# Graph attention on one core: adjacency factors as maxima on VectorE, a bias of 2 in GpSimd's exponentials, and opening zeros in one bf16 pass

## The chip, the cores and the metric

The kernel runs on one core of a Trainium2 chip. The core has engines that work side by side, each through its own queue in order: TensorE (PE in the profile, PEld for its weight loads), VectorE (DVE), ScalarE (ACT), GpSimd (POOL) and SyncE (SP), which here issues nearly all DMAs. Times are device microseconds of one execution; lower is better. A table row "L1272" is line 1272 of the kernel.

## The reference

x is 3327 x 128, adj is a 3327 x 3327 matrix of zeros and ones with ones on its diagonal. Two layers follow each other, each with a residual and a normalisation:

```python
# layer 0: one-head attention with leaky-relu scores, masked by adj
H = X @ W.T + b
e = leaky_relu(A * (H @ a_s) + A * (H @ a_r).T, 0.2)
x = layernorm(x + softmax(where(A > 0, e, NEG), axis=1) @ H)

# layer 1: heads and channels trade places, adj is added twice
q = (x @ Wq.T).reshape(d, n, h)          # d = 128, n = 3327, h = 8
# k and v likewise
a = einsum('dnh,dmh->dnm', q, k) * d ** -0.5 + adj + adj
out = einsum('dnm,dmh->dnh', softmax(a, axis=2), v).reshape(n, h * d) @ Wo.T
x = layernorm(x + out)
```

Layer 1 is nearly all the work: 128 score matrices of 3327 x 3327, an exponential for each of their elements, and a product with 8 value columns. With q scaled by half, the exponent is 2 * (s + adj), where s is the score of the kernel's matmul. So exp(2s + 2 adj) can be had in two ways: add adj to s and take the exponential with a scale of 2; or take exp(2s) and multiply it by a factor that is 1 where adj is 0 and e^2 where adj is 1.

## The kernel before, in words

The function `special` is what runs on these inputs; `general` is a way out for inputs that fail a test of ranges, and is not entered.

**Layer 1's loop.** The 128 matrices are handled in 32 groups of four (HG). The queries are cut into six blocks of 512 and a last one of 256 (`exact`). A pass over one block for one group of four is an entry of `sequence`; two groups share the short last block, side by side in one 512-wide tile ("shared block", `both` in the code, two entries in `s.v4`). So 16 pairs of groups x 13 entries give 208 entries, numbered u.

**One entry.** The keys are cut into 26 tiles of 128 or 127. A tile for four matrices is two "chunks" of 128 x 1024: scores of two matrices each, made by `pair_scores` (called from the loop, recorded under line 155) into a PSUM tile `scb`. Each chunk goes one of two ways:

- POOL's way (`at_ is None`): ScalarE takes exp(2s) from PSUM into SBUF (L1272), and GpSimd multiplies it by the factor (L1273). Its score tile comes from a pool of one buffer.
- DVE's way: VectorE adds adj to the scores (L1275), and ScalarE takes the exponential of both chunks of a tile at once, one round later, in place (`exp_late`, L1059).

Then `products` multiplies the four exponentials with the value columns and accumulates over the 26 tiles in the PSUM tile `av` (L1015), with a lag of five tiles. `av` has one buffer; VectorE copies it out at the end of the entry (L1025) and SP stores it.

**Rounds, stretches and the written order.** The order of all instructions is written out by hand (`manual_schedule`): nothing is moved by a planner afterwards. An entry has 26 rounds, each with two chunks. The rounds fall into "stretches" of three (`plans`, `laid`): a stretch has three tiles, two chunks of one of them go POOL's way, the other four DVE's way. In a stretch ScalarE therefore has two exponentials of 1024 elements and two of 2048. The first stretch of every second entry and the last of every entry are shorter.

**The adjacency tiles.** `want_adj(n)` loads what stretch n needs into a tile `at` with three planes (five buffers, issued three stretches ahead on SP's queue): plane 0 is for POOL's factor, the others are for DVE's additions. The first time that a pair of block and key tile is met (`made_by`), plane 0 holds raw adj, and `make_factor`, called at the end of the stretch before (L1283), turns it in place into 1 or e^2 = adj * (e^2 - 1) + 1 (L840). Whether GpSimd or VectorE does it depends on the stretch's number m in its entry; VectorE's form goes over the row in a strided order of two runs of 256. The result is stored to DRAM (`ftd`, L841, issued through `issue` a few rounds later on SP), and later entries load it from there (L807). There are 7 blocks x 9 = 63 such factors, all made in the first seven entries.

**Opening a shared block's sums.** In a shared block the four matrices of both groups lie side by side in `av`, and each matmul writes one half. `start=True` cannot be given by the halves here, so `products` first issues four matmuls over all 512 columns with a zero weight tile `nought` and the first tile of exponentials as the moving side (L1012), one per band of 32 output rows; all others then accumulate.

**Beside the loop.** Layer 0 for the later row tiles, the projections, the final products and normalisations are put between the rounds as small side jobs by `work` and `work_tensor` (matmuls recorded under L246, VectorE's L337, L419, L425 and others, GpSimd's L319 and L328). The prologue does layer 0 for the first rows; its ScalarE instructions L909, L931, L934 and L937 have a bias that is read per partition, and L941 a scale that is read per partition. ScalarE's L421 there has constants alone.

The constants `nought`, `ones` and the like are made in the pool `keep` before anything else (L195 to L198).

Of the kernel before, what the change touches and what calls it, by code (L numbers as in the profile page):

```python
# [8 lines left out]
F32 = mybir.dt.float32  # L9
F32R = mybir.dt.float32r  # L10
BF16 = mybir.dt.bfloat16
I32 = mybir.dt.int32
AF = mybir.ActivationFunctionType
ALU = mybir.AluOpType
# [3 lines left out]
P = 128  # L18
# [9 lines left out]
E2 = 7.38905609893065  # L28
# [19 lines left out]
def kernel(  # L48
# [27 lines left out]
    nc = tc.nc  # L76
# [24 lines left out]
    W = 512  # L101
# [51 lines left out]
    def special():  # L153
# [9 lines left out]
        with ExitStack() as sx, tc.manual_schedule(engines=ALL):  # L163
            keep = sx.enter_context(tc.tile_pool(name="sx_keep", bufs=1))
# [27 lines left out]
            nc.vector.memset(one_row, 1.0)  # L192
            nrm = keep.tile([1, 4], F32, name="nrm")

            nought = keep.tile([P, 32], F32, name="nought")  # L195
            nc.vector.memset(nought, 0.0)
            ones = keep.tile([P, 1], F32, name="ones")
            nc.vector.memset(ones, 1.0)  # L198

# [60 lines left out]
            def issue(f):  # L260
                pend.append([ISSUE, f])

            def tick(all_=False):
                for p in pend:
                    p[0] -= 1
                while pend and (all_ or pend[0][0] <= 0):
                    pend.pop(0)[1]()
# [561 lines left out]
            def make_factor(n):  # L829
                if n < len(stretches):  # L830
                    u, m = stretches[n]
                    b = sequence[u][1]
                    times, _ = plans[u % 2][m]
                    if times is None or made_by[b, times] != n:
                        return
                    w = exact[b][2]
                    f = adjs[n][:, 0, :w]
                    engine = nc.vector if m % 2 else nc.gpsimd
                    by = f if engine is nc.gpsimd else f.rearrange("p (b a) -> p a b", a=2)
                    engine.tensor_scalar(by, by, E2 - 1.0, 1.0, op0=ALU.mult, op1=ALU.add)  # L840
                    issue(lambda: nc.sync.dma_start(ftd[b][times // 3][:, :w], f))  # L841


# [2 lines left out]
            with ExitStack() as st:  # L846
# [7 lines left out]
                bias = pro.tile([P, 3], F32, name="bias")  # L854
# [36 lines left out]
                def mm():  # L891
                    return pps.tile([P, 512], F32, tag="mm", name="mm")

                b = mm()
                nc.tensor.transpose(b[:, :D], w0[:, :D], ident)
                nc.vector.tensor_copy(w0t, b[:, :D])
                b = mm()
# [6 lines left out]
                b = mm()  # L904
                nc.tensor.transpose(b[:, :P], first["x"], ident)
                nc.vector.tensor_copy(x0T, b[:, :P])
                b = mm()
# [97 lines left out]
            def products(s, i):  # L1005
                if s.left == NT:
                    s.av = pv.tile([P, W], F32, name="av")
                r, e, w = kr[i], s.e.pop(i), s.w
                s.left -= 1
                if s.left == NT - 1 and len(s.v4) > 1:  # L1010
                    for j in range(HG):
                        nc.tensor.matmul(s.av[32 * j : 32 * j + 32, :], nought[:r], e[:r, j, :], start=True, stop=False)  # L1012
                for j in range(HG):
                    for k, v4 in enumerate(s.v4):
                        nc.tensor.matmul(  # L1015
                            s.av[32 * j : 32 * j + 32, k * w : k * w + w],
                            v4[:r, j, i * H1 : i * H1 + 32],
                            e[:r, j, k * w : k * w + w],
                            start=(s.left == NT - 1 and len(s.v4) == 1),
                            stop=(s.left == 0 and k + 1 == len(s.v4)),  # L1020
                        )
                if s.left == 0:
                    o4 = op_.tile([P, W], F32, name="o4")
                    n0, c0, _ = exact[s.b]
                    nc.vector.tensor_copy(o4, s.av)  # L1025
                    for k, g in enumerate(s.gs):
                        for j in range(HG):
                            d = g * HG + j
                            issue(
                                lambda engine=nc.sync, j=j, d=d, at=k * w: engine.dma_start(  # L1030
                                    oT[:, d * N + n0 + c0 : d * N + n0 + w], o4[32 * j : 32 * j + H1, at + c0 : at + w]
                                )
                            )
# [183 lines left out]
            for u, (gs, b) in enumerate(sequence):  # L1217
                if len(gs) == 1:
                    groups = {g: x for g, x in groups.items() if g >= gs[0]}
                s = Block()  # L1220
                s.gs, s.b, s.q4, s.left, s.e, added = gs, b, queries[0], NT, {}, {}
                s.k4, s.v4 = [groups[g][0] for g in gs], [groups[g][1] for g in gs]
                w = s.w = exact[b][2]
                odd, both = u % 2, len(gs) == 2
                rounds, order, starts = plan_of[odd]
                for n, rnd in enumerate(rounds):
                    now = u * NR + n
                    if n in starts:
                        m = number[u, starts[n]]
                        if m:  # L1230
                            want_adj(m + AHEAD)
                        a = adjs[m]
                    tick()
                    for f in soon.pop(now, []):
                        f()
                    if opening < NG:
                        at = begins[opening] - OPEN[opening]
                        if now == at:
                            finish_to(("rows", reads[opening]), None)
                            tick(True)  # L1240
                            groups[opening] = open_group(opening)
                        if now >= at:
                            parts = groups[opening][2]
                            for k, f in enumerate(parts):
                                if now == at + OPEN[opening] * k // len(parts):
                                    f()
                        if now == begins[opening] - 1:
                            opening += 1
                    if u + 1 < len(sequence):
                        if n == NR // 2:  # L1250
                            queries = open_queries(u + 1)
                        if NR // 2 <= n < NR // 2 + HG:
                            queries[1](n - NR // 2)
                    sc = {}
                    for i, h, z in reversed(rnd) if n == 1 and not odd else rnd:
                        sc[i, h] = (pe if z is None else pd).tile([P, 2, 512], F32, name="scb")
                        for k, k4 in enumerate(s.k4):
                            c = slice(k * w, k * w + w)
                            for t in range(2):
                                pair_scores(sc[i, h][: kr[i], t, c], k4, s.q4[:, c], i, kr[i], 2 * h + t, w)  # L1260
                    work_tensor(now, n, odd, both)
                    for i, _, _ in reversed(rnd):
                        if i not in s.e:
                            s.e[i] = sp.tile([P, HG, W], F32, name="e4")
                    for i, h, at_ in rnd:
                        r, z = kr[i], sc[i, h]
                        eh, z = s.e[i][:r, 2 * h : 2 * h + 2, :], z[:r]
                        if both:
                            eh, z = (x.rearrange("p t (k w) -> p (t k) w", w=w) for x in (eh, z))
                        ah = a[:r, at_ or 0, :w].unsqueeze(1).to_broadcast([r, W // w * 2, w])  # L1270
                        if at_ is None:
                            nc.scalar.activation(eh, z, AF.Exp, scale=2.0)  # L1272
                            nc.gpsimd.tensor_tensor(eh, eh, ah, op=ALU.mult)  # L1273
                        else:
                            nc.vector.tensor_tensor(eh, z, ah, op=ALU.add)  # L1275
                            added.setdefault(i, []).append(h)
                    exp_late(now)
                    for i in [i for i, hs in added.items() if len(hs) == 2 or odd and i == NT - 2]:
                        hs = added.pop(i)
                        late.append((now + 1, s, i, 2 * min(hs), 2 * max(hs) + 2))  # L1280
                    if n + 1 in starts or n + 1 == NR:
                        del adjs[m]
                        make_factor(m + 1)  # L1283
                    waiting.append((s, order[n]))
                    multiply(n, odd)
                    work(now, n, odd, both)
# [386 lines left out]
```

## Time and profile before

| | us |
|---|---|
| median of 3 runs | 9910.65 (9908.4 to 9919.17) |
| the profiled execution's own time | 9913.75 |
| its span | 9911.7 |
| ScalarE busy | 9826.0 (99%) |
| TensorE busy | 9247.0 (93%) |
| VectorE busy | 9144.8 (92%) |
| GpSimd busy | 9121.1 (92%) |
| POOL's way, exponential L1272: 3640, mean of one | 1.219 |
| DVE's way, exponential L1059: 3640, mean of one | 2.088 |
| POOL's product L1273: 3640, mean of one | 2.399 |
| DVE's addition L1275: 7176, mean of one | 1.219 |

A line of the groups reads: line, engine, operation, output tile <- input tiles, their shapes, count | busy time in us, mean of one in ns | idle time of the engine just before them, and what ended most of it. A line of the list in order of time reads: start and duration in us, engine, line, operation, tiles and shapes, count, and in brackets the idle time before it and its releaser; neighbours of one kind are merged. A line of the waits reads: who waited <- for whom: us in total, times, longest. Instructions of one engine can overlap in the records: the next one starts before the one in front has left the engine's pipe. Then the durations add up to more than the time, and the step from start to start is what an instruction costs the engine.

### The profile page before, as it was taken

The page shows a single profiled execution, that of the slowest core. Times are in us where ns is not written, and L with a number is a line of the kernel's source. Part 1 is how long each engine was busy: PE and PEld are TensorE (multiplying, and loading weights), DVE is VectorE, ACT ScalarE, POOL GpSimd, SP SyncE. Part 2 cuts the span into 40 slices and gives each one's busy share as a digit, 9 for nine tenths or more (in the row PEclk, how much of TensorE's full clock was granted, in tenths as well). Part 3 has the DMA queues.
Part 4 walks back from the last instruction along what each step waited for, and adds up shares of the span by engine and source line. Part 5 has one row for each costly group of instructions (what it writes and reads, how often), then busy time and mean ns, then how long its engine had stood idle before and what let it go on. Part 6 is the DMA issues. An engine that isn't in the chain of part 4 may idle for free.

```text
span 9911.7 us, 205795 instructions
## 1 busy us (share of the span) xinstructions
PE 9247.0 (93%) x79785; PEld 2990.5 (30%) x79785; DVE 9144.8 (92%) x9996; ACT 9826.0 (99%) x7349; POOL 9121.1 (92%) x4643
## 2 busy tenths in 40 slices
PE   8999999999999999999999999999999999999998
PEld 3323323233232332323223232232322323223232
DVE  8999999999989999999999999999999999998988
ACT  8999999999999999999999999999999999999999
POOL 7999998999889999989998998989998999998888
PEclk9999999999999999999999999999999999999999
DMA  7665555655656556555565655556555565555554
GB/s 215 189 185 171 171 179 163 186 158 171 184 154 180 171 162 186 169 167 173 160 184 166 182 172 168 166 166 183 168 172 174 156 181 171 175 172 156 168 152 135
DMA packets 1344016, 1699.58 MB, mean 171 GB/s; under 512 B 347980, under 2 KB 641782, under 8 KB 1339060
## 3 DMA queue, kind: packets, MB, share of 16 engines
q1 hardware_dynamic: 1341726, 1685.40, 56.7%
q8 instruction: 628, 10.29, 0.4%
q14 instruction: 360, 2.95, 0.1%
q10 hardware_dynamic: 1302, 0.95, 0.0%
HBM read 1581.93 MB, written 103.93 MB: 170 GB/s over the span
## 4 chain that ended last, share of the span: by engine, by line
ACT 51%; PE 20%; issue 11%; POOL 7%; DVE 4%; DMA 1%; SPq 0%; POOLq 0%; DVEq 0%; ACTq 0%
ACT e L1059 36%; ACT e L1272 15%; PE av L1015 9%; PE scb L155 9%; POOL e L1273 7%; DVE e L1275 3%; PE bank L246 2%; DVE o L1025 1%; DMA at<-in_adjT_dram 0%; POOL w L319 0%; POOL w L328 0%; DMA k4b<-kT 0%; SPq L781 0%; PE av L1012 0%; DVE dump L337 0%
## 5 line engine op out<-in xcount | busy, mean ns | idle before, releaser
L1273 POOL TENSOR_TENSOR e<-e,at 128x1024 f32<-128x1024 f32 x3640 | 8678.3, 2399 | 728.5 <-ACT e L1272 685.6
L1275 DVE TENSOR_TENSOR e<-scb,at 128x1024 f32<-128x1024 f32 (+1 forms) x7176 | 8442.1, 1219 | 699.3 <-PE scb L155 542.9
L1059 ACT ACTIVATE e<-e 128x2048 f32<-128x2048 f32 (+2 forms) x3640 | 7599.5, 2088 | 15.3 <-DVE e L1275 14.5
L1015 PE MATMUL av<-e,v4b 128*32 128x512 f32 (+2 forms) x46592 | 5737.0, 572 | 44.1 <-DVE o L1025 25.6
L1272 ACT ACTIVATE e<-scb 128x1024 f32<-128x1024 f32 x3640 | 4435.9, 1219 | 25.3 <-PE scb L155 23.6
L155 PE MATMUL scb<-q4b,k4b 32*128 32x512 f32 (+2 forms) x23296 | 3667.8, 476 | 599.3 <-ACT e L1272 505.9
L155 PEld LDWEIGHTS scb<-q4b,k4b 32*128 32x128 f32 (+1 forms) x23296 | 1657.2, 189 | 5388.0 <-ACT e L1272 3382.1
L1015 PEld LDWEIGHTS av<-e,v4b 128*32 128x32 f32 (+1 forms) x46592 | 1100.9, 108 | 1185.2 <-issue 888.3
L246 PE MATMUL bank<-hsb,w 128*32 128x129 f32 (+1 forms) x5200 | 277.9, 286 | 0.0
L319 POOL TENSOR_SCALAR w<-trow,er 128x129 f32<-128x129 f32 x650 | 234.6, 386 | 23.6 <-DMA trow<-td 22.8
L337 DVE TENSOR_SCALAR_CACHE_REDUCE dump<-a 128x384 bf16<-128x384 f32 (+2 forms) x468 | 247.4, 529 | 0.6
L328 POOL TENSOR_TENSOR w<-w,a 128x384 f32<-128x384 f32 (+3 forms) x225 | 211.1, 938 | 6.1 <-DVE e L1275 6.1
L246 PEld LDWEIGHTS bank<-hsb,w 128*32 128x32 f32 (+1 forms) x5200 | 102.3, 108 | 157.7 <-issue 157.7
L1025 DVE COPY o<-av 128x512 f32<-128x512 f32 x208 | 141.8, 682 | 4.6 <-PE av L1015 4.6
L419 DVE TENSOR_SCALAR hi<-bank 128x256 fp32r<-128x256 f32 (+1 forms) x200 | 83.4, 417 | 10.7 <-DMA kT<-hi 8.6
L246 PE MATMUL bank<-wo,ot 128*32 128x128 f32 x1600 | 85.2, 285 | 0.0
L425 DVE SCALAR_TENSOR_TENSOR lo<-bank,hi 128x256 fp32r<-128x256 f32 (+1 forms) x200 | 83.1, 416 | 0.0
L246 PE MATMUL bank<-wq,x1T 128*32 128x256 f32 x800 | 64.7, 395 | 0.0
L246 PE MATMUL bank<-wk,x1T 128*32 128x256 f32 x800 | 64.3, 393 | 0.0
L246 PE MATMUL bank<-wv,x1T 128*32 128x256 f32 x800 | 63.9, 391 | 0.0
L523 PE MATMUL bank<-ident,o 128*128 128x128 f32 x225 | 52.0, 303 | 0.0
L246 PEld LDWEIGHTS bank<-wo,ot 128*32 128x32 f32 x1600 | 31.5, 108 | 48.5 <-issue 48.5
(140 smaller groups left out, 678.5 us busy)
## 6 DMA issues: line engine op xcount, KB each, us to landing
at<-in_adjT_dram SPq DMA_DIRECT2D x1536, 512.0 KB
at<-ftd SPq DMA_DIRECT2D x1674, 256.0 KB
at<-in_adjT_dram SPq DMA_DIRECT2D x278, 256.0 KB
k4b<-kT SPq DMA_DIRECT2D x124, 415.9 KB
q4b<-qT SPq DMA_DIRECT2D x1532, 32.0 KB
at<-in_adjT_dram SPq DMA_DIRECT2D x192, 224.0 KB
a<-in_adjT_dram SPq DMA_DIRECT2D x50, 504.0 KB
at<-ftd SPq DMA_DIRECT2D x135, 128.0 KB
```

Source lines behind the costliest of these rows:

```text
L155: nc.tensor.matmul(dst, k4[32 * j : 32 * j + H4, first_key(i) : first_key(i) + 2 * r - 1 : 2], q4[32 * j : 32 * j + H4, :nb], start=True, ...
L246: nc.tensor.matmul(dst[c0:c1], w[:, c0:c1], mov, **kw)
L319: nc.gpsimd.tensor_scalar(w, s["t"][:, :, :T3], -LOWEST, e, op0=ALU.min, op1=ALU.max)
L328: nc.gpsimd.tensor_tensor(w, w, s["a"][n][:, c0 - i0 : c1 - i0, :r], op=ALU.mult)
L337: nc.vector.tensor_scalar(z, a, float(k), None, op0=ALU.is_equal, op1=ALU.add, accum_out=even[:, t, at : at + 1])
L419: nc.vector.tensor_scalar(s["hi"][:r], s["b"][:r, :QW], scale, None, op0=ALU.mult)
L1015: nc.tensor.matmul(s.av[32 * j : 32 * j + 32, k * w : k * w + w], v4[:r, j, i * H1 : i * H1 + 32], e[:r, j, k * w : k * w + w], start=(s.l ...
L1025: nc.vector.tensor_copy(o4, s.av)
L1059: nc.scalar.activation(e, e, AF.Exp, scale=2.0)
L1272: nc.scalar.activation(eh, z, AF.Exp, scale=2.0)
L1273: nc.gpsimd.tensor_tensor(eh, eh, ah, op=ALU.mult)
L1275: nc.vector.tensor_tensor(eh, z, ah, op=ALU.add)
```

## The change

Three things change.

1. GpSimd's way. The factor becomes 1 where adj is 1 and e^-2 where adj is 0, which is max(adj, e^-2); and the exponential becomes exp(2s + 2), with the 2 as a bias. The product is the same as before. The bias is given as a tile `two` of one value per partition.
2. Who makes the factor. All 63 are made by VectorE, in the row's plain order. The instruction is given a second operation and an output for the sum over the row (`accum_out=unused`), which nobody reads.
3. The zeros that open a shared block. `nought` is now one row of 512 in bf16, and serves both as the weight (its first 32 columns) and as the moving side; the exponentials are no longer read there.

```diff
-            nought = keep.tile([P, 32], F32, name="nought")
+            nought = keep.tile([1, W], BF16, name="nought")
             nc.vector.memset(nought, 0.0)
+            two = keep.tile([P, 1], F32, name="two")
+            nc.vector.memset(two, 2.0)
+            unused = keep.tile([P, 1], F32, name="unused")
...
                     f = adjs[n][:, 0, :w]
-                    engine = nc.vector if m % 2 else nc.gpsimd
-                    by = f if engine is nc.gpsimd else f.rearrange("p (b a) -> p a b", a=2)
-                    engine.tensor_scalar(by, by, E2 - 1.0, 1.0, op0=ALU.mult, op1=ALU.add)
+                    nc.vector.tensor_scalar(f, f, 1.0 / E2, None, op0=ALU.max, op1=ALU.add, accum_out=unused)
                     issue(lambda: nc.sync.dma_start(ftd[b][times // 3][:, :w], f))
...
                 if s.left == NT - 1 and len(s.v4) > 1:
                     for j in range(HG):
-                        nc.tensor.matmul(s.av[32 * j : 32 * j + 32, :], nought[:r], e[:r, j, :], start=True, stop=False)
+                        nc.tensor.matmul(s.av[32 * j : 32 * j + 32, :], nought[:, :32], nought, start=True, stop=False)
...
                         if at_ is None:
-                            nc.scalar.activation(eh, z, AF.Exp, scale=2.0)
+                            nc.scalar.activation(eh, z, AF.Exp, bias=two[:r], scale=2.0)
                             nc.gpsimd.tensor_tensor(eh, eh, ah, op=ALU.mult)
```

The changed kernel has three lines more at the top and two less in `make_factor`, so L155 and L337 of before are L158 and L340 after, L840 is L841, and L1012, L1015, L1059, L1272, L1273 and L1275 are L1013, L1016, L1060, L1273, L1274 and L1276. In the order written out, VectorE gets the 32 factors that GpSimd had, at the same places between the rounds; GpSimd's products then wait for VectorE's semaphore where they waited for GpSimd's own factor, and SP's stores of those factors too. Nothing else is moved on any queue.

## The prediction

> **What bounds the kernel now.** I read the page first, then the groups with their idle time, the chain, the waits, and two stretches in order of time.
>
> ```profile
> span 9911.7 us, 205795 instructions
> PE 9247.0 (93%) x79785; PEld 2990.5 (30%) x79785; DVE 9144.8 (92%) x9996; ACT 9826.0 (99%) x7349; POOL 9121.1 (92%) x4643
> ACT 51%; PE 20%; issue 11%; POOL 7%; DVE 4%; DMA 1%; SPq 0%; POOLq 0%; DVEq 0%; ACTq 0%
> L1059 ACT ACTIVATE e<-e 128x2048 f32<-128x2048 f32 (+2 forms) x3640 | 7599.5, 2088 | 15.3 <-DVE e L1275 14.5
> L1272 ACT ACTIVATE e<-scb 128x1024 f32<-128x1024 f32 x3640 | 4435.9, 1219 | 25.3 <-PE scb L155 23.6
> ```
>
> ScalarE (ACT) is busy 99% of the span with two kinds of exponential, 3640 of each, and sat idle 41 us in front of them in all; the other engines have 7 to 8% left. The busy sums of the two groups are more than the span, since neighbours overlap, so a group's mean is not what one instruction costs. The step from one start to the next is, and I read it in order of time, where instructions with a scalar read per partition stand early and the plain ones later:
>
> ```profile
> 9.71 0.37 ACT L909 ACTIVATE t<-mm,bias 128x128 f32<-128x128 f32 x1 [5.26 <-PE mm L908]
> 12.67 0.26 ACT L931 ACTIVATE er<-mm,bias 128x3 f32<-128x3 f32 x1 [2.59 <-PE mm L928]
> 12.84 0.26 ACT L934 ACTIVATE hsb<-mm,bias 128x3 f32<-128x3 f32 x1
> 12.98 0.26 ACT L937 ACTIVATE tcol<-mm,bias 128x3 f32<-128x3 f32 x1
> 13.13 0.89 ACT L941 ACTIVATE hsb<-mm,hsb 128x128 f32<-128x128 f32 x3
> 32.42 0.60 ACT L421 ACTIVATE hi<-mm 128x512 fp32r<-128x512 f32 x1 [2.63 <-PE mm L204]
> 53.95 1.02 ACT L1272 ACTIVATE e<-scb 128x1024 f32<-128x1024 f32 x1
> 54.85 1.91 ACT L1059 ACTIVATE e<-e 128x2048 f32<-128x2048 f32 x1
> 56.65 1.02 ACT L1272 ACTIVATE e<-scb 128x1024 f32<-128x1024 f32 x1
> ```
>
> A step of L1272 is 54.85 - 53.95 = 0.90 us, one of L1059 56.65 - 54.85 = 1.80 us; the pair is 2.70 us. 3640 pairs at 2.70 are 9828 us: the whole kernel runs at ACT's pace. Over all neighbouring exponentials the steps exceed the clean ones (0.904, 1.803, and 0.950 for the 1024-wide form of L1059) by 77 us, of which 27 us lie before 410 us. That 77 us is all that better waits can give back.
>
> **Part 1: exp of 2s+2 on GpSimd's chunks (the price).** L1272 before has a constant scale and no bias operand. After, each of its 3640 has `bias=two[:r]`, a scalar per partition read from SBUF: an operand more, on the engine that sets the pace. No other ScalarE instruction changes.
> What does such an operand cost? Two ways, from the rows above. Alone: L421 (512 elements, no such operand) takes 0.60 us and L1272 (1024) 1.02, so 0.42 us per 512 elements, 0.82 ns each, and 0.18 us fixed. L909 (128 elements, bias operand) takes 0.37: less 0.105 for elements it is 0.265 fixed. The operand adds 0.085 us.
> Back to back: L931, L934, L937 with 3 elements follow each other every 0.145 us, and L941 (128 elements, a scale operand) with a mean of 378 ns and three in 0.89 us steps by (0.89 - 0.378)/2 = 0.256, less 0.105 = 0.15. So a step with an operand is elements plus 0.15. Without: L1272 is 0.90 - 0.84 = 0.06 (PSUM source), L1059 is 1.80 - 1.68 = 0.12 (SBUF source). The addition is 0.09 by the like source (L941 reads PSUM too), 0.03 to 0.05 if the source is not what makes the two plain ones differ and the larger is the right base. Nothing shows whether the read can run while a 1.7 us exponential streams in front of it; L941 hid none of it behind 0.1 us. So 0 is the lower end, 0.098 the upper (0.15 against the 0.052 that an element price of 0.828 leaves). I take 0.09, on which the lone and the like-source rows agree: 3640 x 0.09 = +328 us. All of it is on the path, for ACT has no room.
>
> The Trainium skill, "ScalarE: Activation LUTs", section "What ACT_TABLE_LOAD costs", speaks against this edit: a [128,1] pointer operand adds about 93 ns to an ACTIVATE that otherwise has immediates, and neighbours overlap by as much either way. By it the part would be, as an estimate, 3640 x 93 ns = 339 us instead of 328; the lone rows above (0.085) agree nearly.
>
> **Part 2: the zeros that open a shared block.** 16 times (once per pair of groups) four fp32 matmuls with a zero weight come first on the accumulator. What they cost now is in one such place:
>
> ```profile
> 4662.46 1.06 PE L1012 MATMUL av<-e,nought 127*32 127x512 f32 x8 [0.26 <-DVE o L1025]
> 4663.34 1.08 PE L1015 MATMUL av<-e,v4b 127*32 127x256 f32 x16
> 4663.98 2.16 ACT L1059 ACTIVATE e<-e 128x2048 f32<-128x2048 f32 x1
> 4664.36 0.53 PE L155 MATMUL scb<-q4b,k4b 32*128 32x256 f32 x8
> 4666.45 1.03 ACT L1272 ACTIVATE e<-scb 128x1024 f32<-128x1024 f32 x1 [0.30 <-PE scb L155]
> ```
>
> The zeros hold PE for 1.06 us in front of the next scores, and ACT pays: from L1059 at 4663.98 to L1272 at 4666.45 are 2.47 us instead of 1.80. Over the 16 places the excess is 12.1 us, 0.75 each. After, four bf16 matmuls of one row replace eight passes and wait for no e; the accumulator's eviction (L1025) still holds them. No bf16 matmul is in the trace, so 0 to 1.06 us; fp32 takes two instructions each of more than one pass, so I take a quarter, 0.27 us. The 0.79 saved is more than the stall: -12 us, with 0 and -12 as ends.
>
> **Part 3: factors on VectorE alone.** 7 blocks x 9 = 63 factors are made, all before 403 us, and stored and reread later. Now POOL makes 32 and DVE 31:
>
> ```profile
> L840 POOL TENSOR_SCALAR at<-at x32: 407/621/769, 40.2 to 402.4; 128x512 f32<-128x512 f32 x27, 128x256 f32<-128x256 f32 x5
> L840 DVE TENSOR_SCALAR at<-at x31: 421/801/2597, 54.0 to 394.8; 128x512 f32<-128x512 f32 x27, 128x256 f32<-128x256 f32 x4
> 157.59 2.38 POOL L1273 TENSOR_TENSOR e<-e,at 128x1024 f32<-128x1024 f32 x1
> 158.24 2.02 DVE L840 TENSOR_SCALAR at<-at 128x512 f32<-128x512 f32 x1
> ACT e L1272 <- PE scb L155: 13.2, 17, 1.6
> ACT e L1059 <- DVE e L1275: 6.4, 10, 1.6
> ```
>
> (the last two: ACT's waits between 49 and 410 us). DVE's form takes 0.42 us when nothing is in its way and up to 2.6 when POOL runs: at 158.24 it ended 0.29 us after POOL's product did. The new form also writes a sum, so its row is L337's TENSOR_SCALAR_CACHE_REDUCE: 544 ns at 384 elements, 409 at 256, 405 to 555 throughout, with POOL busy beside it; plus 83 ns for reading the sum. At 512: 544 + 135 + 83 = 0.76 us. 63 of them (9 at 256: 0.49) are 45.5 us against 33.4 now: +12 us on DVE; POOL loses 19 us. DVE is late with adds less long at a time, but in every stretch rather than every second. The two ends: all 27 us of stalls before 410 us go, or the 32 new ones of 0.76 us delay the adds and ACT with them, +24 us. POOL's product now waits for DVE's factor; behind it stand POOL's next products and the mask's work. SP's store of the factor waits for DVE instead of POOL, and queued behind it are adj loads wanted three stretches on: covered, since three stretches of two pairs are 16 us. I take -8 us, a third of the stalls there, as DVE's largest hold falls from 2.6 to 0.76 us.
>
> The Trainium skill, "VectorE: DVE Perf Modes", section "What auto-detection actually checks", has a one-source SBUF instruction with an even outermost dimension run two elements a cycle on both ports, which the 2x256 pattern before meets and the 421 ns agrees with. If the new form ran so too, it could be held as now: 63 holds instead of 31, and the saving of this part would be gone.
>
> **Part 4: more room elsewhere.** With 0.09 us more per pair, POOL (2.40 of 2.70 us per pair) and DVE catch up sooner after a burst; of the 38 us of stalls that are left after 410 us I take a fifth: -8 us (ends 0 and -38). Three memsets at the start and the wider zero tile lie beside DMA waits: 0, under 0.3 us if not.
>
> Sum: 328 - 12 - 8 - 8 = +300 us on the profiled execution's own 9913.75 (span 9911.7): **10214 us**. That execution is 3 us above the median of 9910.65, within 0.03%.
>
> **Rivals.**
> - *The operand's read is hidden* behind the 1.7 us exponential in front of it. For it: L941 only ever had 0.1 us in front. Against: L941's 0.1 us would have covered the 0.09, and hid none. Then 9913.75 - 12 - 8 = 9894 us, and 9886 if the factor stage gains twice as much. It ends not slower once the exposed read is below 20 us / 3640 = 5 ns. Chance 0.08.
> - *Half of it shows* (0.046 us, by the larger base): 167 - 28 = +139: 10053 us. Chance 0.06.
> - *VectorE becomes the bound before 410 us*: factors delay the adds by 24 us instead of giving 8, and POOL waits for them. For it: DVE is busy 334 of 361 us there. Against: POOL is as full, and a pair grows by 0.09 us. 10214 + 32 = 10246 us. Chance 0.05.
> - *The zeros do not get shorter* (the four do not run side by side): 10226 us, inside the forecast.
>
> **How the numbers follow.** The forecast has 0.81. Its range: above, 357 us (0.098 each) and only 9 of gains, 10262; below, 310 us (0.085) less 12, 27 and 28 of stalls, 10157. It takes in the VectorE rival; half and hidden, 0.14, are left out. No change and a change are told apart at 0.2%, 20 us. Slower: 0.81 + 0.05 + 0.06 = 0.92; the hidden case's 9886 to 9902 lies across -0.2%: faster 0.05, same 0.03.
>
> **What would show it.** In the profile after, a step of L1273 (the old L1272) should be 0.99 us, the pair 2.79, and ACT still 99% busy, with DVE, PE and POOL down to about 89%. The zeros: some 0.3 us of PE and no 2.4 us step behind them. The factor: 63 on VectorE at 0.68 and 0.08 us, none longer than 0.8. A step of 0.90 at the changed exponential makes the prediction wrong at once; ACT waiting for DVE before 410 us by more than 6.4 us makes part 3 wrong.

## The result, and the profile after

The changed kernel takes 10210.11 us (median of 6 runs, 10207.45 to 10212.34); before, 9911.65 us over 6 runs. The ratio is 1.030, 95% interval 1.0287 to 1.0314. The profiled execution took 10209.42 us, with a span of 10207.6: 295.9 us more than the span before. The forecast was 10214 us.

The page after, its engines, chain and the two exponentials (the score matmuls stand under L155 in both kernels, not under L158):

```profile
span 10207.6 us, 205784 instructions
PE 9230.6 (90%) x79721; PEld 2964.5 (29%) x79721; DVE 9159.5 (90%) x10092; ACT 10145.6 (99%) x7349; POOL 9111.1 (89%) x4611
ACT 59%; PE 16%; issue 15%; POOL 5%; DVE 4%; DMA 1%; SPq 0%; POOLq 0%; DVEq 0%; ACTq 0%
L1060 ACT ACTIVATE e<-e 128x2048 f32<-128x2048 f32 (+2 forms) x3640 | 7861.0, 2160 | 4.5 <-DVE e L1276 4.4
L1273 ACT ACTIVATE e<-scb,two 128x1024 f32<-128x1024 f32 x3640 | 5029.7, 1382 | 8.3 <-PE scb L155 7.3
```

ScalarE is still at 99%; the other three fell from 92 or 93% to 89 or 90%, because the span grew and their work did not. ScalarE's idle time in front of the two exponentials fell from 41 to 13 us, and the kernel is 3% slower all the same. The means mislead here: L1273's grew by 163 ns and L1060's, which was not touched, by 72 ns. In order of time, ScalarE alone, at 5000 us:

```profile
5000.31 1.43 ACT L1273 ACTIVATE e<-scb,two 128x1024 f32<-128x1024 f32 x1
5001.31 2.23 ACT L1060 ACTIVATE e<-e 128x2048 f32<-128x2048 f32 x1
5003.11 1.44 ACT L1273 ACTIVATE e<-scb,two 128x1024 f32<-128x1024 f32 x1
5004.10 2.25 ACT L1060 ACTIVATE e<-e 128x2048 f32<-128x2048 f32 x1
```

From L1273's start to L1060's are 1.00 us, where before it was 0.90; from L1060's to the next 1.80, as before. The medians over the whole trace, to the nanosecond: 997 against 904, and 1801 against 1803. So the changed exponential costs 93 ns more, and the long one beside it nothing. The 104 short ones of L1060 (1024 elements) have a shortest step of 946 ns before and after; their median went from 951 to 1037, and what lies above the clean 950 is counted among the stalls here.

The steps account for the span. 3640 x 93 ns are +338.5 us; 3535 steps shorter by 2 ns are -7.1; the stalls (the sum of all steps less the clean ones, as the prediction counts them) went from 77.2 to 37.5 us, -39.7; the sum is +291.7. The start is 0.5 us and the tail behind the last step 3.7 us longer: 295.9, as measured.

The other two parts, as the lines' own rows show them (count, then shortest/median/longest in ns):

```profile
L841 DVE TENSOR_SCALAR_CACHE_REDUCE at<-at x63: 406/674/682, 47.0 to 394.2; 128x512 f32<-128x512 f32 x54, 128x256 f32<-128x256 f32 x9
L841 DVE DVE_READ_ACCUMULATOR at<-at x63: 78/82/85, 47.6 to 394.5; 128x1 f32 x63
L1013 PE MATMUL av<-nought x64: 371/384/386, 358.6 to 9851.7; 1*32 1x512 bf16 x64
```

All 63 factors are made on VectorE, none longer than 0.68 us, with 0.08 for the sum. The zeros are 64 short matmuls, four per shared block. ScalarE's waits between 49 and 410 us are now:

```profile
ACT e L1273 <- PE scb L155: 6.9, 8, 1.5
ACT e L1060 <- DVE e L1276: 0.2, 1, 0.2
```

### The profile page after: what moved, and what is told of

It reads as the page before. It is cut to its first block, busy times and chain, and to the rows that moved or that the text cites. A ratio compares the mean times of both kernels' runs of the same rounds, so it can differ in the third digit from the quotient of the medians.

```text
span 10207.6 us, 205784 instructions
## 1 busy us (share of the span) xinstructions
PE 9230.6 (90%) x79721; PEld 2964.5 (29%) x79721; DVE 9159.5 (90%) x10092; ACT 10145.6 (99%) x7349; POOL 9111.1 (89%) x4611
## 4 chain that ended last, share of the span: by engine, by line
ACT 59%; PE 16%; issue 15%; POOL 5%; DVE 4%; DMA 1%; SPq 0%; POOLq 0%; DVEq 0%; ACTq 0%
ACT e L1060 43%; ACT e L1273 16%; PE scb L155 7%; PE av L1016 7%; POOL e L1274 4%; DVE e L1276 3%; PE bank L249 1%; DVE o L1026 0%; DVE dump L340 0%; DVE lo L428 0%; DMA at<-in_adjT_dram 0%; DMA k4b<-kT 0%; POOL w L322 0%; PE bank L526 0%; DVE at L841 0%
## 5 line engine op out<-in xcount | busy, mean ns | idle before, releaser
L1274 POOL TENSOR_TENSOR e<-e,at 128x1024 f32<-128x1024 f32 x3640 | 8689.2, 2397 | 1033.7 <-ACT e L1273 977.5
L1276 DVE TENSOR_TENSOR e<-scb,at 128x1024 f32<-128x1024 f32 (+1 forms) x7176 | 8445.5, 1218 | 980.1 <-PE scb L155 836.1
L1060 ACT ACTIVATE e<-e 128x2048 f32<-128x2048 f32 (+2 forms) x3640 | 7861.0, 2160 | 4.5 <-DVE e L1276 4.4
L1016 PE MATMUL av<-e,v4b 128*32 128x512 f32 (+2 forms) x46592 | 5731.9, 571 | 20.5 <-POOL e L1274 2.4
L1273 ACT ACTIVATE e<-scb,two 128x1024 f32<-128x1024 f32 x3640 | 5029.7, 1382 | 8.3 <-PE scb L155 7.3
L155 PE MATMUL scb<-q4b,k4b 32*128 32x512 f32 (+2 forms) x23296 | 3663.8, 476 | 934.7 <-ACT e L1273 894.4
L155 PEld LDWEIGHTS scb<-q4b,k4b 32*128 32x128 f32 (+1 forms) x23296 | 1631.7, 189 | 5745.6 <-ACT e L1273 3797.1
L1016 PEld LDWEIGHTS av<-e,v4b 128*32 128x32 f32 (+1 forms) x46592 | 1098.6, 108 | 1151.4 <-issue 899.1
L340 DVE TENSOR_SCALAR_CACHE_REDUCE dump<-a 128x384 bf16<-128x384 f32 (+2 forms) x468 | 247.1, 528 | 0.6
```

What stands on the lines that cost most here:

```text
L155: nc.tensor.matmul(dst, k4[32 * j : 32 * j + H4, first_key(i) : first_key(i) + 2 * r - 1 : 2], q4[32 * j : 32 * j + H4, :nb], start=True, ...
L340: nc.vector.tensor_scalar(z, a, float(k), None, op0=ALU.is_equal, op1=ALU.add, accum_out=even[:, t, at : at + 1])
L1016: nc.tensor.matmul(s.av[32 * j : 32 * j + 32, k * w : k * w + w], v4[:r, j, i * H1 : i * H1 + 32], e[:r, j, k * w : k * w + w], start=(s.l ...
L1060: nc.scalar.activation(e, e, AF.Exp, scale=2.0)
L1273: nc.scalar.activation(eh, z, AF.Exp, bias=two[:r], scale=2.0)
```

## The experiments

Each is a small edit of the kernel before or after, and is compared with the kernel before on the same chip. The theory was that the operand read from SBUF is the whole loss, an added time per instruction that nothing hides, and that the other two parts gain a little. The rivals: the read is hidden, or VectorE's factors and GpSimd's new wait are what costs.

### The change without the operand

```diff
-                            nc.scalar.activation(eh, z, AF.Exp, bias=two[:r], scale=2.0)
+                            nc.scalar.activation(eh, z, AF.Exp, bias=2.0, scale=2.0)
```

Against the changed kernel.

> The whole change, but the 2 of exp(2s+2) is a constant in the instruction instead of a tile with one value per partition. The operand theory: the price of the change sits in reading that tile, 3640 times some 0.093 us on ScalarE; without it the step from the exponential in front of GpSimd to the next goes back from 0.997 to 0.904 us and the kernel to 9911.7 less the gains of the other two parts: 12 us (zeros) and 8 to 18 us (factors), 9882 to 9895 us. The rival (VectorE's factors, GpSimd's new wait, or the exponential of larger numbers are what costs): it stays near 10210 us with steps of 0.997.

Measured: 9896.16 us (11 runs) against 9912.49 (27 runs), ratio 0.9987 (0.9977 to 0.9996).

```profile
5000.00 2.00 ACT L1060 ACTIVATE e<-e 128x2048 f32<-128x2048 f32 x1
5001.81 1.11 ACT L1273 ACTIVATE e<-scb 128x1024 f32<-128x1024 f32 x1
5002.71 2.01 ACT L1060 ACTIVATE e<-e 128x2048 f32<-128x2048 f32 x1
```

The steps are 903 and 1802 ns at the median. So of the change's +298 us one operand in one instruction is 314, and the rest of it gains 16. The rival falls: the factors on VectorE, GpSimd's waits for them (18.3 us in 21 places) and the larger numbers in the exponential are all still there. The time missed the expected stretch by 1 us: ScalarE's stalls are still 61 us, of which 18.7 lie before 410 us. This kernel beats the one after, and by 16 us (0.13%) the one before.

### The operand alone

```diff
+            zero = keep.tile([P, 1], F32, name="zero")
+            nc.vector.memset(zero, 0.0)
...
-                            nc.scalar.activation(eh, z, AF.Exp, scale=2.0)
+                            nc.scalar.activation(eh, z, AF.Exp, bias=zero[:r], scale=2.0)
```

Against the kernel before.

> The kernel before with one thing added: the exponential in front of GpSimd's product gets a bias tile of one value per partition, all zero, so that the numbers are those of before. The operand theory: 3640 x 0.093 = 339 us on top of 9911.7, less what the other engines' larger room gives back. In the profile after the change the stalls of ScalarE were 77.1 - 28.5 = 48.6 us less; if that came from the slower pace alone, 10202 us; if 20 us of it came from the zeros and the factors, 10222 us. The rival (the operand is read in the shadow of the exponential in front): 9912 us.

Measured: 10219.38 us against 9912.49, ratio 1.0308 (1.0294 to 1.0322), +307 us.

```profile
5000.01 1.46 ACT L1274 ACTIVATE e<-scb,zero 128x1024 f32<-128x1024 f32 x1
5001.00 2.27 ACT L1061 ACTIVATE e<-e 128x2048 f32<-128x2048 f32 x1
5002.81 1.47 ACT L1274 ACTIVATE e<-scb,zero 128x1024 f32<-128x1024 f32 x1
```

The step is 997 ns at the median. The read is not hidden. The time is near the second of the two expected. 338.5 us of price came out as 307, mostly since ScalarE's stalls fell from 77.2 to 53.1 us although zeros and factors were as before: the only thing that changed is the pace, 93 ns more per pair. (The 48.6 us in the expectation take for the short exponentials of the long line each trace's own median; with the clean 950 ns in both it is 39.7 us.) Of these 39.7 us, 24.1 came from the pace and 15.6 (53.1 to 37.5) from zeros and factors. By the medians the changed kernel is 9 us faster than this one, by the profiled executions 16 (10209.42 against 10225.42, the slowest of this kernel's five runs).

### The operand on the long exponential

```diff
-                    nc.scalar.activation(e, e, AF.Exp, scale=2.0)
+                    nc.scalar.activation(e, e, AF.Exp, bias=zero[: kr[i]], scale=2.0)
```

Against the kernel before, with the same zero tile; L1272 as before.

> The kernel before, with the zero bias tile on the other exponential, the late one over both chunks (2048 elements, from SBUF), and none on the one in front of GpSimd's product. If the operand costs the same whatever the length and the source: its step goes from 1.803 to 1.896 us, 3640 x 0.093 = 339 us less some 32 us of stalls: 10219 us. If it can be read in the shadow of a long instruction or of SBUF's longer latency: 1.803 and 9912 us.

Measured: 10219.21 us against 9916.3, ratio 1.0307 (1.0291 to 1.0322). In order of time:

```profile
4999.81 1.46 ACT L1274 ACTIVATE e<-scb 128x1024 f32<-128x1024 f32 x1
5000.71 2.45 ACT L1061 ACTIVATE e<-e,zero 128x2048 f32<-128x2048 f32 x1
5002.63 1.44 ACT L1274 ACTIVATE e<-scb 128x1024 f32<-128x1024 f32 x1
```

The plain one steps by 0.90 us again, and the long one by 1.92 here, with a median of 1894 ns in the trace (before: 1803). Neither length nor source shows in the price: +91 ns at 2048 elements from SBUF, +93 at 1024 from PSUM, and for the 104 short ones of the long line, 1024 elements from SBUF, the shortest step went from 946 to 1039 ns, also +93.

### Two operands

```diff
-                            nc.scalar.activation(eh, z, AF.Exp, scale=2.0)
+                            nc.scalar.activation(eh, z, AF.Exp, bias=zero[:r], scale=two[:r])
```

Against the kernel before, with tiles of zeros and twos.

> The kernel before, with the exponential in front of GpSimd's product reading two tiles of one value per partition: a bias of zero and a scale of two (the numbers are those of before). One such operand made its step 0.997 us instead of 0.904. Theory one, each operand is a read of its own in front of the elements: 1.090 us, 3640 x 0.186 = 677 us, less 32 us or somewhat more of stalls that the slower pace swallows: 10540 to 10560 us. Theory two, one read serves both: 0.997 us and 10219 us.

Measured: 10551.27 us against 9916.3, ratio 1.0639 (1.0623 to 1.0656), +635 us.

```profile
5000.70 1.35 ACT L1276 ACTIVATE e<-scb,zero,two 128x1024 f32<-128x1024 f32 x1
5001.79 2.07 ACT L1063 ACTIVATE e<-e 128x2048 f32<-128x2048 f32 x1
5003.60 1.36 ACT L1276 ACTIVATE e<-scb,zero,two 128x1024 f32<-128x1024 f32 x1
```

The step is 1.09 us (median 1090 ns): 904, 997, 1090 for none, one and two. Each operand is paid for on its own. Of 677 us, 36 went into stalls that are no longer there (77.2 to 41.4).

### The zeros alone

```diff
-            nought = keep.tile([P, 32], F32, name="nought")
+            nought = keep.tile([1, W], BF16, name="nought")
...
-                        nc.tensor.matmul(s.av[32 * j : 32 * j + 32, :], nought[:r], e[:r, j, :], start=True, stop=False)
+                        nc.tensor.matmul(s.av[32 * j : 32 * j + 32, :], nought[:, :32], nought, start=True, stop=False)
```

Against the kernel before.

> The kernel before with the bf16 zeros alone. The stall theory: each of the 16 shared blocks loses 0.75 us on ScalarE now; the zeros go from 1.06 us of TensorE to 0.4 or less; -10 to -12 us, 9900 to 9902 us, and the steps of 2.4 us behind the zeros are gone. The rival (the stall is TensorE's twice as many value products and score matmuls in a shared block, which come right behind, and only shows up there): within 3 us of before, the stall moved to the next step.

Measured: 9903.43 us (11 runs) against 9912.49, ratio 0.9991 (0.9982 to 1.0000): -9 us, at the edge of what can be told from nothing. The trace of it, at the same shared block as in the prediction:

```profile
4654.76 0.40 PE L1012 MATMUL av<-nought 1*32 1x512 bf16 x4 [0.26 <-DVE o L1025]
4655.08 1.09 PE L1015 MATMUL av<-e,v4b 127*32 127x256 f32 x16
4656.10 0.53 PE L155 MATMUL scb<-q4b,k4b 32*128 32x256 f32 x8
```

The value products begin 0.32 us after the zeros began, where it was 0.88. ScalarE's excess at the 16 places fell from 12.1 to 3.7 us. So the stall theory holds for 8.4 us of the 12. That the rest belongs to the rival, a shared block's own matmuls, would fit, but no run shows it.

### The factors alone

```diff
-                    engine = nc.vector if m % 2 else nc.gpsimd
-                    by = f if engine is nc.gpsimd else f.rearrange("p (b a) -> p a b", a=2)
-                    engine.tensor_scalar(by, by, E2 - 1.0, 1.0, op0=ALU.mult, op1=ALU.add)
+                    nc.vector.tensor_scalar(f, f, 1.0 / E2, None, op0=ALU.max, op1=ALU.add, accum_out=unused)
...
-                            nc.scalar.activation(eh, z, AF.Exp, scale=2.0)
+                            nc.scalar.activation(eh, z, AF.Exp, bias=2.0, scale=2.0)
```

Against the kernel before, zeros as before.

> The kernel before with the 63 factors as maxima with an unused sum on VectorE, and exp(2s+2) with the 2 as a constant; the zeros are as before. The hold theory (VectorE's old form was held while GpSimd ran, up to 2.6 us, and that made the adds late): ScalarE's stalls before 410 us fall from 27 to about 10 us, 9895 us. The rival (those stalls went in the changed kernel because the slower pace left room): stalls before 410 us stay within 5 us of 27, 9907 to 9917 us.

Measured: 9904.21 us (11 runs) against 9912.49, ratio 0.9992 (0.9983 to 1.0001): -8 us, again at the edge. ScalarE's stalls before 410 us fell from 26.6 to 18.1 us, 8.5 us, half of what the hold theory named; its waits there for VectorE's additions fell from 6.4 to 1.1 us. With the operand alone, at the slower pace, they fell to 17.4, and with both, in the changed kernel, to 9.2: both theories were partly right, each with 8 to 9 us.

### The factors without the unused sum

```diff
-                    nc.vector.tensor_scalar(f, f, 1.0 / E2, None, op0=ALU.max, op1=ALU.add, accum_out=unused)
+                    nc.vector.tensor_scalar(f, f, 1.0 / E2, None, op0=ALU.max)
```

Against the change without the operand (bias 2.0 as a constant).

> The whole change with the 2 as a constant, as in the run with the constant bias (9896 us), but the 63 maxima on VectorE without the unused sum. The hold theory (the plain form runs at two elements a cycle over ports that GpSimd also uses, and is held while GpSimd runs; the sum takes it out of that mode): a factor takes 0.42 us unhindered and up to 2.6 us, mean about 1 us, ScalarE's stalls before 410 us rise from 18.7 us to 27 or more, and the time to 9904 to 9915 us. The rival (the sum is of no use, only the move to VectorE counts): every factor takes under 0.7 us and the time is 9890 to 9897 us.

Measured: 9912.22 us (11 runs) against 9916.3, ratio 0.9995 (0.9986 to 1.0004), where the same kernel with the sum had 0.9987 (0.9977 to 0.9996) against the kernel before on its chip. The gain is smaller, -4 us for -16, but the two intervals overlap, so the times alone do not settle it. The factor's row of this run:

```profile
L841 DVE TENSOR_SCALAR at<-at x63: 348/673/2317, 47.2 to 402.8; 128x512 f32<-128x512 f32 x54, 128x256 f32<-128x256 f32 x9
```

and of the same kernel with the sum:

```profile
L841 DVE TENSOR_SCALAR_CACHE_REDUCE at<-at x63: 410/677/709, 47.2 to 392.7; 128x512 f32<-128x512 f32 x54, 128x256 f32<-128x256 f32 x9
```

The medians are alike, 673 and 677 ns, so the median tells nothing; the longest is 2317 against 709, and ScalarE's stalls before 410 us are 28.5 against 18.7 us. By these two traces the sum that nobody reads is worth some 10 us: at 512 elements its form took 0.67 to 0.71 us every time, the plain one 0.41 to 0.43 with nothing in its way, but often far more. The longest of the plain ones, and GpSimd beside it:

```profile
75.59 4.70 POOL L1274 TENSOR_TENSOR e<-e,at 128x1024 f32<-128x1024 f32 x2
78.25 2.32 DVE L841 TENSOR_SCALAR at<-at 128x512 f32<-128x512 f32 x1
```

It ends 0.28 us behind the second of GpSimd's products. So do the others that were long: of the 54 with 512 elements, 36 took more than 0.45 us, and each of these ended 0.28 to 0.29 us behind one of GpSimd's instructions, nearly always a product, like the one of the old form in the prediction (0.29). In these traces the plain form is held until GpSimd's running instruction is done, and the form with the sum is not; by what means, no profile shows.

## Why the prediction was right

The forecast of 10214 us is 4 us over the result, but its terms are not as good as their sum.

- *Part 1, the operand: the mechanism and the sign right, the size a little low.* 0.09 us was taken, 0.093 measured: 338.5 us instead of 328. The bounds of 0 and 0.03 to 0.05 fall: the read is not hidden behind 1.7 us of another instruction (step 997), nor behind 0.9 us (step 1894 on the long one). The base by the like source was the right one. The figure set beside it, from the Trainium skill's "ScalarE: Activation LUTs", section "What ACT_TABLE_LOAD costs", with about 93 ns for each pointer operand, agrees with the runs: 93 for one, 186 for two, 91 on the long one. That neighbours overlap by as much either way agrees too: the shortest record of the changed line grew from 999 to 1093 ns, 94 for a step that grew by 93.
- *Part 2, the zeros: taken at -12 us, alone -9.* That the 0.79 us saved would be "more than the stall" did not hold: the four took 0.40 us, not 0.27, and the value products came forward by 0.56 us, less than the 0.75 of the stall.
- *Part 3, the factors: taken at -8 us, alone -8.* The duration was right (0.674 and 0.082 us for 0.68 and 0.08). VectorE did not become the bound: ScalarE waited for its adds 0.2 us before 410 us, where it had been 6.4, and 1.1 us at the old pace with the factors alone. The prediction's condition that the new form could be held like the old one did not come true; the plain form was held, up to 2.32 us.
- *Part 4, the room: mis-sized, -8 us against 24 in the run with the operand alone.* A fifth of the 38 us of stalls after 410 us was taken, and nothing before 410 us for this reason. Measured were 15 of 50.6 us after 410 (to 35.7) and 9 of 26.6 before. The price was 10 us too low and this term 16 us too small; that the sum fits to 4 us is luck: these two, 4 us too many for the zeros, 7 us from long steps that got 2 ns shorter and 4 us more at the start and the tail nearly cancel.
- *The parts add, as the prediction's sum takes it.* Zeros and factors took 16.1 us of stalls away at the old pace (77.2 to 61.1) and 15.6 at the slower one (53.1 to 37.5), and the pace alone took 24.1. In the medians it is 16 us (9896.16 against 9912.49) and 9 (10210.11 against 10219.38); with these intervals the two can't be told apart.
- *The rivals.* Hidden and half hidden have fallen with the steps of 997 and 1894 ns. VectorE as the bound fell with the change without the operand, which is faster than before. That the four zeros don't get shorter fell with their 0.40 us.

What was not tried is where the 93 ns go inside ScalarE; the runs show only that they are added per operand and are the same behind either kind of exponential.

## What to carry to other kernels

On an engine that is 99% busy, look at what an edit adds to each of its instructions, not at the instruction count: one operand read per partition, on half of ScalarE's instructions, was 3% of this kernel, and the same value as a constant in the instruction cost nothing. Read such a price from start-to-start steps, not from mean durations, which grew by 163 ns here for 93 ns of cost. And when an edit makes the bounding engine slower, take off what the slower pace saves by itself: here 24 of 77 us of stalls.

## What was not expected

- The slower pace took 24 us of stalls away by itself (77.2 to 53.1 us with one operand, to 41.4 with two), three times what was forecast.
- An instruction whose extra output is thrown away was better in its place than the plain one: 677 and 673 ns at the median, but 709 against 2317 ns at the longest, and 10 us less of ScalarE's stalls.
- The best kernel of these is the change with its 2 as a constant: 9896.16 us, 0.9987 of before (0.9977 to 0.9996).
